# Cross attention on one core: batch 0's keys by block products, the setup in a written order, and two reads moved

## The chip, the cores and the metric

The kernel runs on one core of a Trainium2 chip. The metric is the time of one execution on the device in microseconds (us); three runs of the kernel before took 945.8, 946.26 and 946.75 us, so the median is 946.26 us. An engine of the core executes its own list of instructions in order; the engines meet only at semaphores. TensorE (PE, with its weight loads PEld) multiplies, VectorE (DVE), ScalarE (ACT) and GpSimd (POOL) work on elements, SyncE (SP) issues most of the transfers.

## The reference

For each of 16 batches, with `x` of 100 rows by 640, `enc` of 718 rows by 384 and `ca` of 4 rows by 384:

```python
query = x @ Wq;  keyt = enc @ Wk;  valt = enc @ Wv          # 8 heads of 80
hs = mha(query, keyt, valt)                                # softmax over 718 keys
ca_q1 = einsum('btc,th->bch', ca, Wq_ca)[:, indices]
ca_hs1 = mha(ca_q1, x, x)                                  # keys and values are x
ca_hs2 = mha(ca_hs1 @ Wq, ca @ Wk_ca, ca @ Wv_ca)          # 4 keys
out = (hs + ca_hs2) @ Wout + b_out + x
```

All is fp32.

## The kernel before, in words

The program is unrolled over the 16 batches. The keys of a batch are kept transposed in `kT` (5 chunks of 128 rows, three thirds of 240 columns), its values in `vs` (six blocks of 120 keys, two halves of four heads each).

Two ways of multiplying a batch's `enc` with a weight exist. The plain way takes all the partial products: `chunk_keys` makes one chunk of keys from 3 thirds by 3 parts of `enc`, nine products of 240 columns (L558), and `first_values` makes one block of values, half by half (L375). The other way, `Keys` and `Values`, multiplies the 3 by 3 parts of `enc` with 3 by 2 parts of the weight by 15 block products instead of 18 (`V_PLAN`, `K_PLAN`). It needs sums of parts: `enc_sums` makes 13 sums per batch on GpSimd (L500), `weight_sums` makes 12 sums per weight (L521). `Blocks.go(n)` issues the next n products (L434 for values, L465 for keys); after each product the bank's running sum is copied to its place by ScalarE (L407) or added there by VectorE (L405), and only then may the next product go into that bank. The fifth chunk of the keys is always made the plain way (`last_keys`).

**The setup** (L266 to L1104) is ordered by the tile scheduler, except for transfers marked `in_order`. SyncE loads `enc` of batch 0 (thirds 1 and 2), `cat`, `Wk_ca`, `Wq` transposed (L295), third 0 of `enc`, `x` transposed, `cas`, `Wk` transposed in nine transfers (`load_packed`, L302), `Wq` (L308) and `Wv_ca` (L309); ScalarE's queue loads `Wv` (L282). TensorE makes four blocks of batch 0's values (L375), the small keys `k2` (L1005) and from them `m` (L1028), the first `y_ps` (L739), the transposes of `Wk` (L1051), batch 0's keys the plain way (`first_keys`, L558), `va` (L1083) and the first queries (L534). Banks of PSUM come from three pools of two: `psumk`, `psum1`, and pairs of banks; `psum` alternates between the first two. VectorE masks `k2` (L1017), copies `m` out (L1036), sorts `Wq` into place (L1062, L1069) and makes the weight sums (seven and five of Wk, seven of Wv). GpSimd builds masks and expands `m` (L711, `keys`), then forms the first products of the second attention (L774, L781).

**The loop** (L1116) runs in an order written out by hand (`manual_schedule`, L1115). Batch b makes scores in three tiles `st[0]` to `st[2]` of two key blocks each (L613; copies L630 and L624), a running maximum (L1150), then subtracts (L1138) and exponentiates (L1146) each tile. Between them TensorE makes the products of values b and keys b+1. In batch 0 two blocks of values are still made the plain way, and GpSimd makes the last five sums of Wv (L1205). Then `a_ps` (L1301) multiplies the exponentials with the values: two groups of four heads, head by head, each over all six key blocks, in two column parts. The result is divided by the row sums. In batch 1 the second attention's part is added to batch 0's result by one VectorE instruction (L1166), which stands between the scores' maxima; then `last.transpose()` (L1210, L916) turns that sum for the last projection.

Of the kernel before, what the change touches and what calls it, by code (L numbers as in the profile page):

```python
# [132 lines left out]
def kernel(  # L133
# [62 lines left out]

    def hsT_tile(name):
        return main.tile([P, HC, P], F32, tag="hsT", name=name, bufs=2)
# [81 lines left out]
    for g in range(2):  # L280
# [6 lines left out]
    load_first(0, CC, 2, slice(0, KT))  # L287
    tokens = vb_tile("tokens")
# [3 lines left out]
    in_order(nc.sync.dma_start(out=wkca_sb, in_=wkca.rearrange("(c p) n -> p c n", p=P)))  # L292
    wqt_sb = wout_sb
    wkt_sb = kT.rearrange("p c u k -> p c (u k)")
    in_order(nc.sync.dma_start(out=wqt_sb, in_=wqt.rearrange("(c p) r -> p c r", p=P)))  # L295
    load_first(0, CC, 0, slice(0, KT))
# [4 lines left out]
    load_packed(  # L301
        lambda **ends: in_order(nc.sync.dma_start(**ends)), wkt_sb[:, :, :CAD], wkt  # L302
    )
# [45 lines left out]
    m_sb = [t[:, : B * HT] for t in (hs_tile("m_0"), xn_tile("m_1"), xn_tile("m_2"))]  # L349
# [60 lines left out]
    class Values(Blocks):  # L410
# [17 lines left out]
        def product(self, at, f, first, last):  # L428
# [4 lines left out]
            for j in range(2):  # L433
# [3 lines left out]
                    wv_sb[:, W_AT[f]],  # L437
# [43 lines left out]
    def enc_sums(enc):  # L481
# [3 lines left out]
        for out, left, right, op in (  # L485
            (at(11), raw(3, 2), raw(3, 3), ALU.add),
# [5 lines left out]
            (at(7), raw(2, 3), raw(3, 1), ALU.add),  # L492
# [9 lines left out]
    def weight_sums(engine, w, late):  # L502

        at = lambda f: w[:, W_AT[f]]
        raw = lambda c, g: w[:, 2 * (c - 1) + g - 1]
        for out, left, right in (
            (at(5), raw(2, 2), raw(1, 2)),
            (at(14), raw(2, 1), raw(2, 2)),
            (at(7), raw(3, 2), at(5)),
            (at(3), raw(1, 1), at(7)),  # L510
            (at(13), raw(3, 1), at(7)),
        ) if late else (
            (at(0), raw(1, 2), raw(1, 1)),
            (at(1), raw(2, 1), raw(3, 1)),
            (at(2), raw(1, 1), raw(2, 2)),
            (at(6), raw(2, 1), raw(1, 1)),
            (at(10), raw(3, 1), raw(2, 2)),
            (at(11), raw(2, 2), raw(3, 2)),
            (at(12), raw(3, 2), raw(3, 1)),
        ):  # L520
            engine.tensor_tensor(out, left, right, ALU.subtract)  # L521
# [8 lines left out]
    def queries(p, xT, tiles, n):  # L530
        qp, qz = tiles
        q_ps = psum(f"q_ps_{p}_{n}")
# [42 lines left out]

    def first_keys(enc):
        for n in range(HC - 1):
            banks = [psum(f"kT_ps_0_{n}_{k}") for k in range(2)]
            weights = [wk_sb[:, 2 * c + n % 2, n // 2] for c in range(CC)]
            chunk_keys(n, banks, weights, enc)  # L580
        last_keys(0, enc)
# [136 lines left out]
    class Second:  # L718
# [135 lines left out]
        def values2(self, behind=None):  # L854

            b, p2, vb = self.b, self.p2, self.vb
            self.hs2 = main.tile([S, H], F32, tag="hs2", name=f"hs2_{b}")
# [24 lines left out]
    class Last:  # L882
# [26 lines left out]
        def transpose(self, chunks=[(0, HC)]):  # L909
            b, hs = self.b, self.hs  # L910
            if not self.t_ps:
                self.t_ps = psumk(f"hst_ps_{b}")
# [83 lines left out]

    for i in (1, 4, 2, 5):
        first_values(i, enc, (act, dve))
# [14 lines left out]
    for n, heads in enumerate(HEADS):  # L1013
# [10 lines left out]
        )  # L1024
    for c in range(HC):
# [10 lines left out]
        copied = nc.vector.tensor_copy(  # L1036
# [6 lines left out]
    summed = second.products()  # L1043
# [3 lines left out]

    for c in range(HC):
        w_ps = psum(f"w_ps_{c}")
        for cc in range(CC):  # L1050
            nc.tensor.transpose(  # L1051
                w_ps[:, cc * P : (cc + 1) * P], wkt_sb[:, c, cc * P : (cc + 1) * P], ident
            )
        act(
            wk_sb[:, c % 2 : 6 : 2, c // 2] if c < HC - 1 else wk4,
            w_ps[:, : CC * P].rearrange("p (a n) -> p a n", a=CC),
        )

    with tc.issue_after(summed.ins):
        for c in range(HC):  # L1060
            for u in range(2):
# [317 lines left out]
```

## Time and profile before

| what | us |
|---|---|
| median of three runs | 946.26 (945.8 to 946.75) |
| the profiled execution | 945.6 |
| its span, first to last instruction | 943.9 |
| PE busy in it | 935.4 |
| granted TensorE clock | 0.999 |
| DVE, POOL, ACT busy | 680.7, 626.0, 361.8 |
| start of the first scores (L613) | 60.24 |

The profile is of one execution. Its span leaves out 1.7 us that the device time includes. Times of places are in us from the span's start. A product in fp32 stands in the trace as two matmul records, so "x4" in a row of products is two products. Durations of matmuls overlap in the records; how long one takes in a chain is read from starts, or from the chain of work that ended last, where each piece has its own share of time.

### The profile page before, as it was taken

To read this page: it belongs to the slowest core of one execution; us is meant where nothing else is said; L and a number is where in the kernel's file an instruction comes from. 1 tells how busy PE (TensorE), PEld (TensorE's weight loads), DVE (VectorE), ACT (ScalarE), POOL (GpSimd) and SP (SyncE) were. 2 spreads that over 40 slices of the span, in tenths; PEclk is the share of its full clock that TensorE was granted. 3 is DMA by queue.
4 is the path that set the end of the run, shared out by engine and by line. 5 is a ranking of instruction groups with operands and counts; after the bars stand their busy time and mean duration, and the time that the engine had idled before them with its cause. 6 is when DMAs were issued, how large, how long until landed. Compare 5 with 4: busy or idle time off the path is not lost.

```text
span 943.9 us, 25613 instructions
## 1 busy us (share of the span) xinstructions
PE 935.4 (99%) x11215; PEld 796.8 (84%) x11215; DVE 680.7 (72%) x1083; ACT 361.8 (38%) x598; POOL 626.0 (66%) x570
## 2 busy tenths in 40 slices
PE   9999999999999999999999999999999999999998
PEld 6997879788797888978789887987989888897866
DVE  1869794877929778595965959579693886949683
ACT  1234433524324244433424434244431534334241
POOL 4649978776737766595872948657694576848523
PEclk9999999999999999999999999999999999999999
DMA  8822014040320404004050030403113030210200
GB/s 269 268 95 87 3 48 135 1 130 3 88 65 1 116 2 118 23 2 130 1 151 3 28 91 1 138 2 94 38 38 115 1 111 8 57 55 1 94 8 29
DMA packets 45367, 62.48 MB, mean 66 GB/s; under 512 B 13448, under 2 KB 37320, under 8 KB 43656
## 3 DMA queue, kind: packets, MB, share of 16 engines
q1 hardware_dynamic: 41720, 42.97, 15.3%
q0 software_dynamic: 2512, 16.72, 6.0%
q8 instruction: 88, 1.44, 0.7%
q10 hardware_dynamic: 1024, 1.15, 0.4%
q14 instruction: 23, 0.19, 0.1%
HBM read 55.26 MB, written 5.57 MB: 64 GB/s over the span
## 4 chain that ended last, share of the span: by engine, by line
PE 95%; DVE 3%; ACT 1%; DMA 0%; issue 0%; POOL 0%; ACTq 0%; DVEq 0%
PE s_ps L613 12%; PE a_ps L1301 12%; PE v_psA L434 10%; PE v_psB L434 9%; PE kT_ps L558 7%; PE k_psA L465 7%; PE q_ps L534 7%; PE o_ps L944 7%; PE k_psB L465 6%; PE v_psC L434 3%; PE k_psC L465 2%; PE v_psD L434 2%; PE v_psE L434 2%; PE y_ps L739 2%; PE v_ps L375 1%; PE k_psE L465 1%
## 5 line engine op out<-in xcount | busy, mean ns | idle before, releaser
L774 POOL TENSOR_TENSOR e<-ca,g 100x800 f32<-100x800 f32 x64 | 99.5, 1565 | 132.4 <-DVE most L1150 128.7
L863 POOL TENSOR_TENSOR hs<-vb,p 100x640 f32<-100x640 f32 x64 | 105.0, 1650 | 40.1 <-DVE p L849 32.0
L870 POOL TENSOR_TENSOR hs<-hs,hs 100x640 f32<-100x640 f32 x48 | 115.1, 2398 | 3.8
L1301 PEld LDWEIGHTS a_ps<-vs,st 120*64 120x64 f32 (+3 forms) x3072 | 109.0, 125 | 6.9 <-issue 5.5
L1301 PE MATMUL a_ps<-vs,st 120*64 120x81 f32 (+3 forms) x3072 | 112.1, 234 | 1.0 <-ACT st L1146 1.0
L434 PE MATMUL v_psA<-wv_sb,enc 128*120 128x320 f32 x360 | 112.0, 434 | 0.0
L1138 DVE TENSOR_TENSOR st<-st,over 120x1600 f32<-120x1600 f32 x48 | 108.2, 2255 | 0.0
L500 POOL TENSOR_TENSOR enc<-enc 128x240 f32<-128x240 f32 x135 | 99.2, 749 | 7.1
L630 ACT COPY st<-s_ps 120x800 f32<-120x800 f32 x64 | 49.7, 829 | 135.9 <-PE s_ps L613 135.9
L613 PE MATMUL s_ps<-qp,kT 32*120 32x100 f32 x3072 | 97.4, 263 | 0.0
L613 PEld LDWEIGHTS s_ps<-qp,kT 32*120 32x120 f32 x3072 | 94.7, 179 | 1.6 <-issue 0.2
L781 POOL TENSOR_TENSOR e<-e,e 100x800 f32<-100x800 f32 x48 | 92.3, 1923 | 3.8
L434 PE MATMUL v_psB<-wv_sb,enc 128*120 128x320 f32 x300 | 93.1, 433 | 0.0
L465 PE MATMUL k_psA<-enc,wk_sb 128*128 128x240 f32 x360 | 87.6, 366 | 0.0
L1312 DVE RECIPROCAL rs<-a_ps 100x4 f32<-100x4 f32 x32 | 5.8, 182 | 112.9 <-PE a_ps L1301 112.9
L434 PEld LDWEIGHTS v_psA<-wv_sb,enc 128*120 128x120 f32 x360 | 64.5, 183 | 23.0 <-issue 0.5
L1150 DVE TENSOR_TENSOR most<-most,st 120x800 f32<-120x800 f32 x64 | 65.7, 1027 | 23.6 <-ACT st L624 22.5
L1146 ACT ACTIVATE st<-st 120x1600 f32<-120x1600 f32 x48 | 73.8, 1539 | 23.2 <-DVE st L1138 23.2
L465 PEld LDWEIGHTS k_psA<-enc,wk_sb 128*128 128x128 f32 x360 | 68.3, 190 | 16.7
L500 POOL TENSOR_TENSOR enc<-enc,rest 128x240 f32<-128x240 f32 x45 | 33.9, 752 | 68.3 <-DMA rest<-in_enct 36.0
L434 PEld LDWEIGHTS v_psB<-wv_sb,enc 128*120 128x120 f32 x300 | 54.8, 183 | 22.1 <-DVE vs L405 0.4
L465 PE MATMUL k_psB<-enc,wk_sb 128*128 128x240 f32 x300 | 73.1, 366 | 0.0
(137 smaller groups left out, 1765.7 us busy)
## 6 DMA issues: line engine op xcount, KB each, us to landing
vb<-va_d POOLq DMA_DIRECT2D x16, 1000.0 KB, 7.3
enc<-in_enct SPq DMA_DIRECT2D x30, 240.0 KB, 3.8
enc<-in_enct SPq DMA_DIRECT2D x15, 360.0 KB, 3.5
xT<-in_xt SPq DMA_DIRECT2D x8, 500.0 KB, 4.6
rest<-in_enct SPq DMA_DIRECT2D x31, 120.0 KB, 6.1
xn<-in_x SPq DMA_DIRECT2D x11, 320.0 KB, 5.3
out<-xn SPq DMA_DIRECT2D x11, 320.0 KB, 3.1
ca<-in_cas SPq DMA_DIRECT2D x16, 156.2 KB
```

Source lines behind the costliest of these rows:

```text
L434: nc.tensor.matmul(at[0][j][:KN, : H // 2], a_form(self.enc, f)[:, j * KN : (j + 1) * KN], wv_sb[:, W_AT[f]], start=first, stop=last, skip ...
L465: nc.tensor.matmul(at[:, i * KT : (i + 1) * KT], wk_sb[:, W_AT[f], i], a_form(self.enc, f), start=(first and i == 0), stop=last, skip_grou ...
L500: nc.gpsimd.tensor_tensor(out, left, right, op)
L534: nc.tensor.matmul(q_ps[:, : 2 * S].rearrange("p (j s) -> p j s", j=2), wq_sb[:, c, n * P : (n + 1) * P], xT[:, :, c, :], start=(c == 0), ...
L613: nc.tensor.matmul(s_ps[r][:n, 256 * a + lo : 256 * a + hi], kT[rows, c, u, j * KN : (j + 1) * KN], rhs, start=(a == 0 and c == 0), stop=( ...
L774: first = nc.gpsimd.tensor_tensor(to, self.ca[:, t, :].unsqueeze(1).to_broadcast([S, NH, S]), g[:, :, t].unsqueeze(2).to_broadcast([S, NH, ...
L781: nc.gpsimd.tensor_tensor(e, e, to, ALU.add)
L863: first = nc.gpsimd.tensor_tensor(to, vb[:S, t, :].rearrange("p (h d) -> p h d", h=NH), p2[:, :, t].unsqueeze(2).to_broadcast([S, NH, D]), ...
L870: nc.gpsimd.tensor_tensor(sums, sums, to, ALU.add)
L1138: return nc.vector.tensor_tensor(st[i], st[i], top.over[:KN].unsqueeze(1).to_broadcast([KN, 2, ROWS]), ALU.subtract,)
L1146: nc.scalar.activation(st[i], st[i], AF.Exp, scale=SCALE)
L1301: nc.tensor.matmul(a_v[lo:hi, h % 4], st[i // 2][: KEYS[i], i % 2, h * S + lo : h * S + hi], block(i, h // 4)[: KEYS[i], h % 4], start=(i ...
```

## The change

- `Wq` transposed is loaded by ScalarE's queue, issued after the fourth copy of values; SyncE loads third 0 of `enc` before `cat`, and `Wk` transposed ahead of `x` transposed, `cas` and `Wq`.
- The hand-written order begins before the first values. All their copies are ScalarE's.
- `enc_sums` for batch 0 stands in the setup, and `f=7` is made first. All 12 sums of Wv are made by VectorE in the setup; three of them (5, 14, 7) go to spare room (`wv_there`, in `bias` and a tile of `xn`), and ScalarE copies them into `wv_sb` late in batch 1, after which the bias is loaded. GpSimd's five sums in batch 0 are gone.
- The transposes of `Wk` come before `m`, ScalarE copies `m` out, all sums of Wk follow on VectorE at once, then the sorting of `Wq`.
- Batch 0's keys are made by 15 block products, `k0.go(3)`, then `y_ps`, then `go(4)`, `va`, and two after each of the first four query chunks; `last_keys` stands before the last query chunk. `va` and the queries take pairs of banks.
- In the first group of `a_ps` the order is by tiles of scores: all four heads over `st[0]`, then `st[1]`, then `st[2]`.
- In batch 1 the addition of `hs2` stands after `y_ps` of the next batch, and the transposes after three value and three key products, in a bank of `psum1`.

```diff
     load_first(0, CC, 2, slice(0, KT))
+    load_first(0, CC, 0, slice(0, KT))
...
+    load_packed(
+        lambda **ends: in_order(nc.sync.dma_start(**ends)), wkt_sb[:, :, :CAD], wkt
+    )
     wqt_sb = wout_sb
-    in_order(nc.sync.dma_start(out=wqt_sb, in_=wqt.rearrange("(c p) r -> p c r", p=P)))
-    load_first(0, CC, 0, slice(0, KT))
...
-    load_packed(
-        lambda **ends: in_order(nc.sync.dma_start(**ends)), wkt_sb[:, :, :CAD], wkt
-    )
...
+    room_v = xn_tile("wv_there")
+    wv_there = {5: bias[:, : H // 2], 14: bias[:, H // 2 :], 7: room_v[:, : H // 2]}
...
-    q_ps = psum(f"q_ps_{p}_{n}")
+    q_ps = get(f"q_ps_{p}_{n}")
...
+    ctx.enter_context(tc.manual_schedule(engines=engines))
     for i in (1, 4, 2, 5):
-        first_values(i, enc, (act, dve))
+        first_values(i, enc, (act, act))
+        if i == 4:
+            nc.scalar.dma_start(out=wqt_sb, in_=wqt.rearrange("(c p) r -> p c r", p=P))
+    enc_sums(enc)
+    weight_sums(nc.vector, wv_sb, there=wv_there)
...
+    for c in range(HC):
+        w_ps = psum(f"w_ps_{c}")
...
+    weight_sums(nc.vector, wk_sb)
...
-        copied = nc.vector.tensor_copy(
+        nc.scalar.copy(
             m_sb[c].rearrange("p (b h t) -> p h b t", h=NH, t=T),
...
+    k0 = Keys(0, enc)
+    k0.go(3)
+    second.products()
     second.copy()
     second.scores1()
     keys(load_m(1))
...
-    first_keys(enc)
-    weight_sums(nc.vector, wk_sb, True)
+    k0.go(4)
...
-    va_ps = psum("va_ps")
+    va_ps = bank("va_ps")
...
     for n in range(HC):
-        queries(0, xT, tiles, n)
-    nc.gpsimd.dma_start(out=bias, in_=bout[0].partition_broadcast(P))
+        queries(0, xT, tiles, n, bank)
+        k0.go(2)
+        if n == HC - 2:
+            last_keys(0, enc)
...
-        if b == 1:
-            nc.vector.tensor_tensor(last.hs[:S], last.hs[:S], last.hs2, ALU.add)
         st.append(scores(b, 2, tiles))
 
         now.softmax2()
         if b + 1 < B:
             second.products()
             second.copy()
+        if b == 1:
+            nc.vector.tensor_tensor(last.hs[:S], last.hs[:S], last.hs2, ALU.add)
...
-            weight_sums(nc.gpsimd, wv_sb, True)
...
-            last.transpose()
+            if b > 1:
+                last.transpose()
...
+            if b == 1:
+                last.transpose(get=psum1)
...
+            if b == 1:
+                for f in list(wv_there):
+                    nc.scalar.copy(wv_sb[:, W_AT[f]], wv_there.pop(f))
             second.load()
+            if b == 1:
+                nc.gpsimd.dma_start(out=bias, in_=bout[0].partition_broadcast(P))
...
-            for h in range(4 * g, 4 * g + 4):
...
+            order = [(h, i) for h in range(4 * g, 4 * g + 4) for i in range(len(KC))]
+            if g == 0:
+                order.sort(key=lambda at: at[1] // 2)
+            for h, i in order:
```

## The prediction

> **What bounds the kernel now.** I read the page first: busy time of each engine, then the granted clock by slice.
>
> ```profile
> PE 935.4 (99%) x11215; PEld 796.8 (84%) x11215; DVE 680.7 (72%) x1083; ACT 361.8 (38%) x598; POOL 626.0 (66%) x570
> ...
> PEclk9999999999999999999999999999999999999999
> ```
>
> TensorE is busy for 935.4 of 943.9 us at full clock. So only two things can save time: fewer products, or less of the 8.5 us in which PE is idle or winding up. Next I read what PE waited for over the whole span:
>
> ```profile
> PE hst_ps L916 <- DVE hs L1166: 1.3, 1, 1.3
> PE idle_ps L994 <- DVE idle L991: 1.1, 1, 1.1
> PE a_ps L1301 <- ACT st L1146: 1.0, 1, 1.0
> PE m_ps L1028 <- DVE wq L1017: 0.5, 1, 0.5
> PE y_ps L739 <- POOL m L711: 0.4, 1, 0.4
> PE k_psC L465 <- DVE kT L405: 0.3, 1, 0.3
> ```
>
> All of these lie in the first 112 us; batches 2 to 15 have no wait of PE to win. Apart from the start (1.1) they add up to 3.5 us. Last, the chain of work in the setup:
>
> ```profile
> 21.27 6.91 PE m_ps L1028 x50
> ...
> 31.66 18.23 PE kT_ps L558 x90
> 49.89 1.76 PE va_ps L1083 x12
> 51.65 8.66 PE q_ps L534 x50
> ```
>
> From 30 us to the first scores (60.24) PE runs without a gap, so what is taken from PE there is won, as long as nothing it needs is late.
>
> **Fewer products.** `first_keys` makes 4 chunks of 9 products and the fifth chunk 9 more: 45 products, 90 records, 18.23 us, so 0.405 us each. The 36 become 15 plan steps of 2 products, 30. A block product has the same 240 columns and the same price: a row of two, k_psA x4, takes 0.81 in the chain of batch 1. Six products fewer: **-2.43 us**. This is certain if the waits do not grow.
>
> **Waits removed.**
> - `m` waits 0.47 for the masks of `k2`, `y_ps` 0.40 for GpSimd. Now the transposes of Wk (15 records, some 2.05 us by their starts) stand between `k2` and `m`, and the masks need 1.2; between `m` and `y_ps` stand three plan steps (2.43), and the last expansion of `m` needs ScalarE's copy (0.69 on VectorE before) and 0.3 on GpSimd. **-0.87**.
> - `a_ps`: before, PE ran 16 records on `st[0]` and `st[1]` and stood 1.02 for `st[2]`. With all four heads over two tiles first, 64 records at 36.4 ns (6.41 us for 176) lie ahead of `st[2]`: from 92.51 to 94.84, and that tile was ready at 94.27. **-1.02**, with 0.5 of cover. The pairs of column parts alternate as before, so I put the new order itself at nothing; it touches 16 groups of 3.5 us, and one per cent either way would be 0.56.
> - `hst_ps`: the transposes now follow 5.7 us of products, and the addition (1.31) ends well within that. But PE then is 1.3 us nearer to VectorE's additions: that of v_psA ended at 120.56 and its next product began at 121.86, so the cover becomes about nil. I keep **-1.1** of 1.31; 0.5 at worst.
> - The wait of k_psC (0.34) stays: the order there is the same.
>
> **Waits added.** Three, all in the setup.
>
> (1) *The last transfer of Wk transposed.* In the built program each transfer waits for the one eight places before it on the shared semaphores; the ninth of Wk (the fifth chunk) waits for Wq transposed. Behind it on SP stand `x` transposed, `cas`, `Wq`, `Wv_ca`; on PE the fifth transpose, then `m` and all that follows. ScalarE issues Wq transposed after its fourth copy (12.48 + 0.42): about 12.9, instead of 8.45. Now the rates:
>
> ```profile
> 10.00:15.00 5.00, 5.00 (x21) 3.36 (x20) 0.49 (x1) 0.85 (x2) 2.24 (x6) 1.00 0.99 377
> ...
> 20.00:24.00 4.00, 3.53 (x48) 3.39 (x45) 1.91 (x6) 0.00 (x0) 0.29 (x1) 1.00 0.94 204
> 24.00:28.00 4.00, 4.00 (x32) 4.00 (x32) 2.07 (x3) 0.00 (x0) 0.98 (x3) 1.00 0.39 103
> ```
>
> The last column is GB/s. Ahead of Wk transposed are `enc` 1.11, Wv 0.98, `cat` 0.10 and Wk_ca 0.98 MB, 3.17 in all; 1.91 had moved by 10 us (191 GB/s), the rest at 377 ends at 13.4. Then come Wk transposed (0.98) and Wq transposed (1.64) together. Here a rule speaks against the change: the Trainium skill, "DMA: Bandwidth & Descriptors", "Issuing engines are not separate DMA queues", says that transfers started on different queues run on the same 16 engines and interleave, so a second queue saves only issue time. So ScalarE's queue brings nothing by itself, and Wq transposed slows Wk. By the rule the sum of bytes counts: 2.62 MB at 377 is 7.0 us, ending at 20.4. By the row in which Wk's packets ran (204, transfers into 32 partitions) it is 12.8 us, ending at 26.2. I take the first: in that row SP stood still, 5.2 us for Wq transposed and 2.3 for `x`, so few transfers were in flight, while now seven are issued ahead. The ninth is then issued at 20.4 and lands 2.6 to 3.2 us later (what the 60 KB loads took): 23.0 to 23.6. PE, done with `k2` at 20.85, has done four transposes by 22.5. Wait 0.5 to 1.1: **+0.8**. By the row it would be 6.6.
>
> (2) *VectorE's additions to kT.* These stand behind the sums of Wk and the sorting of Wq. Sums: 12 by 0.345 from about 23.2, to 27.4; `k0` begins at 30.9 and is covered. Sorting: it took 13.2 us (30.36 to 43.58), because GpSimd's long products ran alongside:
>
> ```profile
> 35.69 0.21 DVE L1069 COPY wq_sb<-wq 128x128 f32<-128x128 f32 x1
> 35.83 1.82 DVE L1062 COPY wq_sb<-wq 128x256 f32<-128x256 f32 x2
> 37.57 1.90 DVE L1069 COPY wq_sb<-wq 128x128 f32<-128x128 f32 x1
> ```
>
> The same copy takes 0.21 or 1.90: a blocked one waits for one whole GpSimd instruction (1.6 to 1.9). Now those products come after `g`, which VectorE makes after the sorting; only the expansions of `m` (0.3 each) run beside it. So 3.3 us alone, 5 with them, to about 32.4, if Wq has landed: 1.64 MB and 0.68 for `x` and `cas` behind 20.8, at 377, is 29. `y_ps` ends at 34.6, so 2 us of cover. What remains is that A's third product waits for VectorE's addition of its second: **+0.2** (0 to 0.8).
>
> (3) *The pair for the first scores.* Queries now take pairs of banks. The built program shows the second pair of the scores waiting for ScalarE's two masked copies of the last query chunk. They took 0.74 after that chunk's end (60.34 to 61.08); before, scores began at once, since queries lay in other banks. PE can do four records, so **+0.75** (0.3 to 1.2).
>
> What is put at nothing: VectorE's 12 sums of Wv (0.40 each, 8 to 13 us; masks needed at 20.85; doubled, still in time); GpSimd's 13 sums of batch 0 (0.75 each, 11.9 to 21.7; first needed at 30.9; at twice the price the last ends near 31, and the expansions are the next late thing); four more copies and `m` on ScalarE, which was 13% busy or less there; its three copies in batch 1, ahead of `st[2]`, behind which 8.5 us of queries stand on PE; the bias load after them on GpSimd, needed in batch 2. The sums of Wv gone from GpSimd (7.34 us in batch 0) were on no path of PE: nothing.
>
> **The sum**: -2.43 - 0.87 - 1.02 - 1.1 + 0.8 + 0.2 + 0.75 = -3.67. The first scores begin about 1.3 us earlier in effect; the rest comes in batches 0 and 1. The profiled execution would take 945.6 - 3.67 = 941.9 (its span 940.2); it lay 0.66 below the median, so the median becomes 942.6. With all favourable ends the gain is 2.43 + 0.87 + 1.02 + 1.31 + 0.33 - 0.3 = 5.7, 940.6.
>
> **Rivals.**
> - *A: the setup gives it back.* If the two transposed weights end at 23 instead of 20.4, wait (1) is about 3.3: 942.6 + 2.5 = 945.1. For it: the window at 204. Against: the window at 377.
> - *B: VectorE late.* Additions to kT now end near 53, then the first softmax's 8.3 us beside GpSimd's sums of batch 1, so VectorE is free near 62, and it is needed for the maxima at 63.6; before, it idled 5.6 us there. If it is 1.5 us late, exponentials are late, `a_ps` loses its 1.0 again and batch 1 0.8: 944.4.
> - *C: slower.* Wq transposed lands at 26.2 or later, by the row. Then the ninth transfer lands at 29.1 and PE stands 6.6: -3.67 + 5.8 = +2.1, 948.4. It decides from a landing of Wq transposed at about 26. A pause that long may cost more: the skill's "TensorE: Matmul & The Clock Gate", "HAM oscillation — how this bites in real kernels", tells of a lower clock after idle gaps of over some 3.4 us; the longest gap here is 1.3 at a clock of 0.999, so no row shows it.
>
> **Chances.** Forecast 0.62, A 0.15, B 0.12, C 0.11. I call a change of over 0.2% (1.9 us) told apart from none, about what a measurement of this kernel can do: below 944.4 faster, above 948.2 slower. Faster: 0.60 of the forecast, 0.05 of A, half of B: 0.71. Slower: most of C, 0.09. The rest, 0.20, is within. The range 940.8 to 946.0 holds the forecast's bounds, A and B.
>
> **What would show it.** 30 products at L470 and none of the plain chunks but the fifth before the first scores; no wait of `hst_ps` on L1174 nor of `a_ps` on the exponentials; a wait of w_ps on the load of Wk near 22.5, of under 1.1; a wait of s_ps on ScalarE of some 0.75; first scores near 59. Wrong would make it: a wait of w_ps over 3 us, rows of `wq_sb` copies of 1.6 us or more, `a_ps` longer than 36.4 ns a record in its first groups, or a wait of PE in the later batches.

## The result and the profile after

The changed kernel takes 953.09 us (median of four runs, 950.3 to 954.28); the kernel before, 946.09 beside it. The ratio is 1.0071 with an interval of 1.0059 to 1.0083, so it is 5.6 to 7.9 us slower. The profiled execution took 953.05 us, with a span of 951.3 (before 943.9). The page of the changed kernel, engines and clock:

```profile
PE 937.2 (99%) x11203; PEld 798.1 (84%) x11203; DVE 672.5 (71%) x1088; ACT 367.7 (39%) x608; POOL 624.5 (66%) x578
...
PEclk9799999999999999999999999999999999999999
```

There are 12 records fewer on PE, as six products fewer must give, and yet PE is busy 1.8 us longer. The clock row says why: its second slice, about 24 to 48 us, has a 7. PE did less work, but some of it at a lower clock. The waits of PE in the changed kernel:

```profile
PE w_ps L1040 <- DMA kT<-in_wkt: 6.8, 3, 3.3
...
PE k_psE L470 <- DVE vs L410: 0.9, 1, 0.9
PE s_ps L612 <- ACT qz L552: 0.5, 1, 0.5
...
PE k_psA L470 <- DVE kT L410: 0.2, 1, 0.2
```

The waits of `hst_ps`, `a_ps`, `m_ps` and `y_ps` are gone, as intended. In their place PE stands 6.8 us for Wk transposed, in three pieces: 3.27 us before the transposes that start at 23.73, 0.50 before those at 25.73, and 3.05 before the fifth chunk's at 30.30. What the loads waited for is in SyncE's own queue, for the first 45 us:

```profile
SPq L299 <- DMA wout_sb<-in_wqt: 8.1, 1, 8.1
...
SPq L299 <- DMA tokens<-in_wkca: 3.6, 1, 3.6
```

L299 is the loading of Wk transposed. Its seventh transfer stood 3.6 us for the landing of `Wk_ca` (16.76), so that the seventh and eighth were issued at 16.78 and 17.54, and its ninth stood 8.1 us for that of Wq transposed. The chain of work that ended last shows the second of these from end to end (start, duration, what):

```profile
12.14 13.78 DMA wout_sb<-in_wqt
...
25.94 4.31 DMA kT<-in_wkt
...
30.30 0.90 PE w_ps L1040 x3
31.20 9.12 PE m_ps L1051 x50
```

Wq transposed was under way for 13.78 us; of its 640 packets only 14 began in the last two of them. Only then was the ninth transfer issued, of 192 KB; it took 4.31 more, and `m` could begin at 31.20 instead of 21.27. The 50 records of `m` then took 9.12 us, where they took 6.91 before. The windows of the same kernel (last three columns: granted clock, share of DMA, GB/s):

```profile
10.00:15.00 5.00, 5.00 (x20) 3.40 (x19) 3.13 (x7) 1.28 (x3) 4.88 (x13) 1.00 1.00 274
15.00:18.00 3.00, 3.00 (x13) 2.05 (x12) 0.00 (x0) 0.85 (x2) 2.84 (x5) 1.00 1.07 181
18.00:20.00 2.00, 2.00 (x54) 1.55 (x54) 0.00 (x0) 0.43 (x1) 1.84 (x4) 1.00 1.05 288
20.00:24.00 4.00, 0.73 (x18) 0.62 (x15) 1.22 (x5) 0.00 (x0) 3.15 (x5) 0.83 0.87 275
24.00:28.00 4.00, 2.75 (x12) 1.98 (x10) 0.20 (x1) 1.92 (x4) 0.00 (x0) 0.50 0.11 17
...
32.00:36.00 4.00, 4.00 (x17) 4.00 (x17) 1.52 (x7) 0.59 (x1) 0.41 (x1) 0.50 1.01 386
36.00:40.00 4.00, 4.00 (x31) 4.00 (x31) 2.04 (x9) 1.76 (x3) 1.03 (x3) 0.97 1.02 397
```

The DMA engines are fully busy from 10 to 20 us and yet move only 181 to 288 GB/s; from 24 to 28 us, with the end of Wq transposed and the start of the ninth transfer, next to nothing moves. The clock falls while PE stands: by the trace's list of clocks it is one half from 22.62 to 36.27 us. From 32 to 36 us PE makes 17 records, where the next four microseconds hold 31.

**Where the time went.** The first scores start at 67.73 instead of 60.24, 7.5 us later. Of that: waits for Wk +6.8; `m`, mostly at half clock, +2.2 (9.12 - 6.91); the transposes without their waits 3.9 us instead of 1.7, +2.3; the wait of `m` -0.5; from the end of `m` to the end of `y_ps` 0.96 us instead of 1.82, -0.9; the keys' pieces of the chain 16.1 us instead of 18.23, -2.1; the small keys start 0.3 earlier. These sum to +7.5. Then batch 0 is 0.8 us shorter (39.60 instead of 40.40), batch 1 as long as before (58.74 and 58.62), and batches 2 to 15 are 0.6 longer, for a cause that stays open.

That batch 1 is no shorter, though `hst_ps` waits no more, is told by the chain through it:

```profile
117.36 1.15 DVE hs L1174
118.51 0.91 DVE most L1152
119.42 0.02 issue
119.44 1.38 DVE most L1152
...
128.94 0.66 DVE kT L410
...
130.95 1.08 PE k_psE L470 x4
```

The addition that was moved (`hs`, 1.15 us) still stands on VectorE ahead of two maxima. From there the chain of what ended last stays with VectorE for over ten microseconds, to its additions to `kT` at 128.94 and to `vs` at 130.52; PE's product of k_psE, which stood 0.92 us for the latter, begins at 130.95. The wait of 1.30 us was not removed; as 0.25 and 0.92 it moved from the transposes to the additions.

### The profile page after: what moved, and what is told of

It reads as the page before. It is cut to its first block, busy times and chain, and to the rows that moved or that the text cites. A ratio compares the mean times of both kernels' runs of the same rounds, so it can differ in the third digit from the quotient of the medians.

```text
span 951.3 us, 25636 instructions
## 1 busy us (share of the span) xinstructions
PE 937.2 (99%) x11203; PEld 798.1 (84%) x11203; DVE 672.5 (71%) x1088; ACT 367.7 (39%) x608; POOL 624.5 (66%) x578
## 4 chain that ended last, share of the span: by engine, by line
PE 93%; DVE 3%; DMA 2%; issue 0%; ACT 0%; ACTq 0%; DVEq 0%
PE s_ps L612 12%; PE a_ps L1313 12%; PE v_psA L439 10%; PE v_psB L439 8%; PE k_psA L470 8%; PE q_ps L540 7%; PE o_ps L943 7%; PE k_psB L470 6%; PE kT_ps L564 6%; PE v_psC L439 3%; PE k_psC L470 3%; PE y_ps L738 2%; PE v_psD L439 2%; PE v_psE L439 2%; DMA wout_sb<-in_wqt 1%; PE k_psE L470 1%
## 5 line engine op out<-in xcount | busy, mean ns | idle before, releaser
L1313 PEld LDWEIGHTS a_ps<-vs,st 120*36 120x36 f32 (+3 forms) x3072 | 109.2, 125 | 5.6 <-issue 5.5
L1313 PE MATMUL a_ps<-vs,st 120*36 120x81 f32 (+3 forms) x3072 | 111.9, 233 | 0.0
L505 POOL TENSOR_TENSOR enc<-enc 128x240 f32<-128x240 f32 x144 | 104.9, 738 | 7.5
L439 PE MATMUL v_psA<-wv_sb,enc 128*120 128x320 f32 x352 | 109.6, 434 | 0.0
L470 PE MATMUL k_psA<-enc,wk_sb 128*128 128x240 f32 x384 | 93.7, 367 | 0.3 <-DVE kT L410 0.2
L470 PEld LDWEIGHTS k_psA<-enc,wk_sb 128*128 128x128 f32 x384 | 72.5, 190 | 17.8 <-POOL e L780 0.7
L470 PE MATMUL k_psB<-enc,wk_sb 128*128 128x240 f32 x320 | 77.9, 366 | 0.0
L540 PE MATMUL q_ps<-xT,wq_sb 128*128 128x200 f32 x400 | 69.7, 333 | 0.0
```

The costliest lines, as they stand in the source:

```text
L439: nc.tensor.matmul(at[0][j][:KN, : H // 2], a_form(self.enc, f)[:, j * KN : (j + 1) * KN], wv_there.get(f, wv_sb[:, W_AT[f]]), start=first ...
L470: nc.tensor.matmul(at[:, i * KT : (i + 1) * KT], wk_sb[:, W_AT[f], i], a_form(self.enc, f), start=(first and i == 0), stop=last, skip_grou ...
L505: nc.gpsimd.tensor_tensor(out, left, right, op)
L540: nc.tensor.matmul(q_ps[:, : 2 * S].rearrange("p (j s) -> p j s", j=2), wq_sb[:, c, n * P : (n + 1) * P], xT[:, :, c, :], start=(c == 0), ...
L1313: nc.tensor.matmul(a_v[lo:hi, h % 4], st[i // 2][: KEYS[i], i % 2, h * S + lo : h * S + hi], block(i, h // 4)[: KEYS[i], h % 4], start=(i ...
```

## The experiments

The theory was: the loss is one of order. Two weights share the DMA engines, the order in which they land is not the order in which PE needs them, and the wait that follows lowers the clock as well; the block products and the loop's new order are innocent. The rivals were that the narrow transfers of Wk are too slow whatever the order, that the clock costs nothing of its own, and that the loop part is worth nothing.

**1. Wq transposed behind Wk transposed**, on SyncE:

```diff
+    in_order(nc.sync.dma_start(out=wqt_sb, in_=wqt.rearrange("(c p) r -> p c r", p=P)))
...
-        if i == 4:
-            nc.scalar.dma_start(out=wqt_sb, in_=wqt.rearrange("(c p) r -> p c r", p=P))
```

> The changed kernel, but Wq transposed is issued by SyncE behind the nine transfers of Wk transposed, so the two don't run at once and no transfer of Wk waits for it. Theory (the two streams slowed each other on the same engines, and the ninth transfer was held by Wq transposed): the wait of the first transposes falls from 3.3 us to under 1, that of the fifth from 3.0 to under 0.5, and a wait of m for Wq transposed of 2 to 3 us appears at some 25 us; the clock stays at 1.00 or nearly; time 945 to 947. Rival (the nine transfers into 32 partitions are slow by themselves): the transposes still wait 3 us and more, Wq transposed lands later than 26, time 952 or more.

It took 948.9 us (948.63 to 949.12, six runs), ratio to before 1.0029 [1.0017, 1.0040]. The waits of its PE, and its windows:

```profile
PE m_ps L1050 <- DMA wout_sb<-in_wqt: 3.5, 1, 3.5
...
PE w_ps L1039 <- DMA kT<-in_wkt: 0.3, 1, 0.3
```

```profile
24.00:28.00 4.00, 0.89 (x4) 0.92 (x5) 3.72 (x11) 0.16 (x1) 0.00 (x0) 0.68 1.04 379
28.00:32.00 4.00, 4.00 (x17) 4.00 (x17) 0.63 (x3) 0.59 (x1) 0.29 (x1) 0.50 1.02 341
```

And the chain of work that ended last:

```profile
9.54 9.08 DMA tokens<-in_wkca
...
19.81 7.16 DMA wout_sb<-in_wqt
...
27.11 9.33 PE m_ps L1050 x50
```

4.2 us of the 7 are won back by this one line, less than the theory asked (945 to 947). Wk is there just in time; now `m` waits 3.5 us for Wq transposed, and the half clock follows that wait as well. The chain shows why Wq transposed is late: SyncE could issue the eighth transfer of Wk only when `Wk_ca` had landed (18.62), then the ninth, and Wq transposed behind it. From 16 to 20 us the DMA engines had a share of 0.31 and moved 72 GB/s; Wq transposed alone then went at 379. So what one weight gains in order, the other loses. The rival is not excluded: with no Wq transposed beside them, Wk's packets took 107 ns on average from 14 to 18 us, where 65 is the least. Nor does the run, which changes the queue and the order of Wq transposed together, tell these two apart.

**2. Wk transposed in five transfers into 128 partitions** (instead of nine into 32 or fewer):

```diff
-    for r, u in [(r, u) for r in range(RG) for u in range(2)]:
-        load(
-            out=to[32 * r : 32 * r + 32, 2 * u : 2 * u + 2],
-            in_=rows[r, u, :64].rearrange("(j p) n -> p j n", j=2),
-        )
+    for u, j in [(u, j) for u in range(2) for j in range(2)]:
+        load(out=to[:, 2 * u + j], in_=rows[:, u, 32 * j : 32 * j + 32])
```

> The changed kernel, but Wk transposed comes in five transfers into all 128 partitions instead of eight into 32 and one into 128, the same bytes. Theory with narrow transfers as the ones that load few engines and drag Wq transposed along: all of Wk lands by about 20, Wq transposed by about 21, waits of the transposes under 1 us in all, clock 1.00, time 944 to 946. Rival (two queues at once are slow whatever their shape): waits of 4 us and more stay, time 950 or more. Here the fifth transfer also doesn't stand behind Wq transposed on a semaphore, so the first wait (3.3) tells the shape, the last one (3.0) may go for either reason.

It took 953.79 us, ratio 1.0083 [1.0069, 1.0097]: nothing won, and `w_ps` waits 8.6 us. By the time that is the rival. But in these transfers the outermost dimension of the source is 4, and from 16 to 30 us mostly 19 to 45 of their packets began in a microsecond, 65 to 126 ns each, as if few engines took part. The Trainium skill, "DMA: Bandwidth & Descriptors", "Rules for kernel authors", says that an outermost dimension of fewer than 16 keeps a transfer to at most that many engines; the run agrees. So this did not test what it was meant to test, the width of the destination, and leaves theory and rival where they were.

**3. PE kept at work**: zero products ahead of the first and the fifth transpose (their results are unused).

```diff
+    warm_ps = bank("warm_ps")
+    warm(14)
     for c in range(HC):
+        if c == HC - 1:
+            warm(14)
```

> The changed kernel with 14 products of zeros (about 3.0 us) ahead of the first and 14 ahead of the fifth transpose of Wk, so TensorE isn't idle while it waits for the load. Theory (the idle time lowered the clock to half from 24 to 36 us): the clock stays at 1.00, m takes 6.9 us again instead of 9.1, time 949.5 to 951, 2 to 3.5 us less than the changed kernel. Rival (m was slow because of what it reads or of the transfers beside it): m stays at 9.1, time within 0.5 of the changed kernel or more.

The median is 951.42 us, but the four runs lie between 948.86 and 954.58, ratio 1.0067 [1.0050, 1.0084]: by the times not told apart from the changed kernel. The zero products kept the clock up in only two of the four: these were granted 1.000 on average and took 948.86 and 950.76, the other two 0.998 and took 952.08 and 954.58 (the changed kernel's four: 0.993 to 0.996). The profiled execution was the shortest of them (span 946.5). Its clock is 1.00 in every window from 20 to 40 us, `m` began at 29.37, and the first scores started at 63.38, 4.35 us earlier. It shows that the clock follows PE's idling, not the size of the gain.

**4. The loop part alone**: the setup of before, with the new order of `a_ps`, and the addition and transposes of batch 1 moved as in the change.

```diff
+            order = [(h, i) for h in range(4 * g, 4 * g + 4) for i in range(len(KC))]
+            if g == 0:
+                order.sort(key=lambda at: at[1] // 2)
...
+            if b > 1:
+                last.transpose()
...
+            if b == 1:
+                last.transpose(get=psum1)
```

> The kernel before with only the two changes in the loop: the first group of the product with V by tiles of scores, and in batch 1 the later sum with the transposes after three products of each. As predicted: the waits of a_ps (1.0) and hst_ps (1.3) go, 944.0 to 944.6 (0.1 to 0.5 us returned by VectorE's additions in batch 1). Rival (what the changed kernel's trace suggests: batch 1 gives it back in two new waits of 0.25 and 0.9): 945.0 to 945.4.

946.36 us (21 runs), ratio 1.0004 [0.9997, 1.0010]: neither the theory's number nor the rival's. The waits of `a_ps` and `hst_ps` are gone, and a new one stands first among the causes in its profile:

```profile
PE k_psA L465 <- POOL enc L500: 2.2, 1, 2.2
```

Batch 2's keys wait for GpSimd's sums of `enc`: with the transposes out of the way, PE comes to them sooner than their pair, the seventh in GpSimd's list, is made. The profiled execution (948.86) is one of the slowest of the 21: right after this wait its clock was one half for 3.41 us, and its first values were slow, so that the first scores started at 61.67.

**5. The loop part, with that pair first in the list:**

```diff
+            (at(7), raw(2, 3), raw(3, 1), ALU.add),
...
-            (at(7), raw(2, 3), raw(3, 1), ALU.add),
```

> The changed kernel's loop part alone, as before (a_ps by tiles, the first sum and its transposes later, setup as it was), now with its order of GpSimd's sums as well: the pair of batch 2's first key chunk is added first. Theory (the 2.2 us that the earlier loop-only run lost at batch 2's keys came from that pair being added seventh, and the later sum wins little because batch 1 waits for VectorE's additions instead): the wait of k_psA on GpSimd falls under 0.5 us, a_ps's 1.0 us is won, of the 1.1 us of hst_ps at most 0.5; 944.6 to 945.4. Rival (the loop part is worth nothing, whatever the order of the sums): 945.8 to 946.4, with another wait of 1 us or more in batches 1 or 2.

943.69 us (11 runs), ratio 0.9977 [0.9968, 0.9985]. One line in the order of 13 sums decides whether the loop part is worth 2.2 us, by the ratio, or nothing. It is worth slightly more than I expected. Its profiled execution was one of its longer ones (945.89), and shows waits of 0.92 and 0.75 us on VectorE's additions in batch 1; run 12 returns to them.

**6. Run 1 with PE kept at work** by zero products ahead of `m`:

```diff
+    warm_ps = bank("warm_ps")
+    for _ in range(16):
+        nc.tensor.matmul(warm_ps[:, :P], idle, idle, start=True, stop=True)
```

> The kernel of the run with Wq transposed issued behind Wk transposed, plus 16 products of zeros ahead of m (extra work, its result unused) that fill the time in which TensorE waits for Wq transposed. Theory (the clock: a wait of 3.5 us makes m and what follows run at a clock of one half for several us): the clock stays at 0.95 or above in every stretch from 20 to 40 us, m takes 6.9 us instead of about 9, the first scores come about 2.2 us earlier than in that run (61.6 instead of 63.85), and the time is 946.2 to 947.0. Rival (the lower clock costs nothing that the later stages would not give back): 948.4 to 949.2, as without the zeros.

947.81 us, ratio 1.0013 [1.0005, 1.0021], with runs from 945.34 to 950.23; the interval overlaps that of run 1. All 20 executions were granted 0.999 or 1.000, where run 1's had 0.996 to 0.998. In the profile the clock is 1.00 in every window from 20 to 40 us, and `m` takes 6.84 us instead of 9.33 with no other change in what it computes. About half of the expected gain shows in the median. The profiled execution, at 949.59 one of the slow ones, tells where a gain can go: the loads ended later (the small keys waited 1.2 us for `Wk_ca`, Wk transposed another 1.3), so `m` began 2.0 us later than in run 1. The half clock has a price of its own, 2.5 us for `m`; that the loads' scatter explains the other executions is not shown, since each run has one trace.

**7. The whole change with loads and setup in the order of before**: SyncE loads Wq transposed ahead of Wk, and `m` precedes the transposes.

```diff
-        if i == 4:
-            nc.scalar.dma_start(out=wqt_sb, in_=wqt.rearrange("(c p) r -> p c r", p=P))
+    in_order(nc.sync.dma_start(out=wqt_sb, in_=wqt.rearrange("(c p) r -> p c r", p=P)))
...
+    for c in range(HC):
+        w_ps = psum(f"w_ps_{c}")
...
+    weight_sums(nc.vector, wk_sb)
+    last_keys(0, enc)
```

> The whole change, but with the order of the loads and of TensorE's setup as before: Wq transposed by SP ahead of Wk transposed, m first, then Wk's transposes, their sums, the last key chunk, then y and the queries. The keys by block products, the sums of Wv in setup and the loop's new order stay. Theory (the loss is the order in which the two weights are needed against the order in which they land, with the clock behind it, and not the block products): no wait of w_ps or m_ps above 1 us, clock 0.95 or above from 20 to 40 us, first scores at 59.5 to 60.2, 944.0 to 945.3. Rival (the block products' setup itself has no cover, since Wk's transposes now stand ahead of the last keys): TensorE waits 2 us or more for Wk transposed or its copies whatever the order, 947 or above.

944.32 us (22 runs), ratio 0.9983 [0.9974, 0.9991]: 8.8 us less than the changed kernel. No wait on Wk or Wq transposed is left, the clock is 1.00 throughout, and the first scores start at 57.92, 2.3 us before those of the kernel before. So the loss lay in the order, that of the loads with their queue and that of PE's setup, which this run turns back together, and not in the block products. These waits are left in its profile where gain was expected:

```profile
PE z_ps L801 <- issue: 1.2, 2, 1.0
...
PE kT_ps L565 <- ACT wk L1060: 1.0, 1, 1.0
PE k_psE L471 <- DVE vs L411: 0.9, 1, 0.9
PE m_ps L1039 <- issue: 0.5, 1, 0.5
PE s_ps L613 <- ACT qz L553: 0.5, 1, 0.5
```

Those of `kT_ps`, for ScalarE's copy of the last transposed chunk of Wk, and of `m` come with the old order of the setup; no run takes them away.

**8. Two of these waits attacked**: the last query chunk in the other pool of PSUM, and batch 1's addition on GpSimd.

```diff
-        queries(0, xT, tiles, n, bank)
+        queries(0, xT, tiles, n, bank if n < HC - 1 else psum1)
...
-            nc.vector.tensor_tensor(last.hs[:S], last.hs[:S], last.hs2, ALU.add)
+            nc.gpsimd.tensor_tensor(last.hs[:S], last.hs[:S], last.hs2, ALU.add)
```

> As the run with the order of before, and two edits more: the last chunk of batch 0's queries in a bank of the other pool of PSUM, and batch 1's second addition to its first sum on GpSimd instead of VectorE. Theory (the 0.45 us ahead of the first scores is a wait for the eviction of the query chunk whose bank they take, and the 0.25 and 0.92 us of batch 1's keys are waits for VectorE, which stands in that addition): the three waits fall under 0.2 us each, and the time is 1.0 to 1.6 us below that run, 943.0 to 944.3. Rival (the waits move to the next instruction on the same engine): within 0.4 us of that run.

947.07 us, ratio 1.0008 [0.9999, 1.0016]: 2.75 above run 7 and worse than the rival's number. In the profile both waits went, and `hst_ps` now stands 2.44 us for GpSimd's addition, while 0.85 us of an unexplained stop appear in the scores. GpSimd was no free place. That profile is of one of the two fastest of 14 executions (945.0, clock 1.000). The other twelve were granted 0.997 or 0.998 and took 946.05 to 949.1; one stretch at half clock like that of run 4, 3.41 us, would make 0.998. So the new stop seems to cost most executions the clock as well, which no trace shows.

**9. The stop without a releaser.** In the profiles of runs 6, 7 and 8 PE stops for 0.85 to 1.02 us with the releaser "issue" (nothing that the profile shows), at recorded instruction 961 or 1218 of its stream. I lengthened its program at the start by 84 instructions:

```diff
-    for _ in range(5):
+    for _ in range(2):
         nc.tensor.matmul(idle_ps[:, :P], idle, idle, start=True, stop=True)
+    for _ in range(24):
+        nc.tensor.matmul(
+            idle_ps[:32, :32], idle[:32, :32], idle[:32, :32], start=True, stop=True
+        )
```

> The kernel of the run with the order of before, with TensorE's program 84 instructions longer at its very start (two of the five zero products that open it stay, 24 small zero products are added in the time in which it waits for its first weights; their results are unused). In three profiles TensorE stands 0.85 to 1.02 us in the middle of the small products of batch 0's first scores and first softmax with no releaser, at recorded instruction 961 or 1218 of its stream, 257 apart, and each packet of the instruction queue has 16,384 bytes. Theory (it stands there for the next block of its own instructions, whose fetch is late beside the loads): the blocks now end 84 instructions earlier in the work, the wait of z_ps at 67.5 us goes or falls under 0.3 us, and the time is 0.7 to 1.1 us below that run: 943.2 to 943.7. Rival (the wait belongs to those products themselves): it stays at the same product, 944.0 or above.

944.69 us, ratio 0.9981 [0.9973, 0.9989]: no gain in time, against the theory's number and within the rival's. The profile splits it. The stop of `z_ps` is gone, and batch 0 takes 39.98 us instead of 40.86; but the first values began 1.3 us late behind my zero products and ran slowly, so that the small keys start at 20.44 instead of 18.31. What I won in one place I had paid in another.

**10. The shift and the other pool for the last query chunk** together:

```diff
-        queries(0, xT, tiles, n, bank)
+        queries(0, xT, tiles, n, bank if n < HC - 1 else psum1)
```

> As the shifted kernel, with the last chunk of batch 0's queries in a bank of the other pool of PSUM. Theory: the 0.45 us of s_ps ahead of the first scores goes, since those scores no longer take the bank of a chunk that has still to be evicted: first scores without a wait above 0.1 us, 942.7 to 943.3. Rival (the wait moves to the next scores or to an instruction block): within 0.2 us of the shifted kernel.

944.64 us, ratio 0.9983 [0.9977, 0.9990], the same as run 9: the rival again. The 0.45 us of the first scores is gone, and 0.26 and 0.34 us appear behind it, on ScalarE's copies of scores and on VectorE.

**11. The addition and transposes later still**, in addition to run 10:

```diff
-        if b == 1:
-            nc.vector.tensor_tensor(last.hs[:S], last.hs[:S], last.hs2, ALU.add)
...
-            if b == 1:
-                last.transpose(get=psum1)
...
             exponential(1)
             vv.go(1)
             kk.go(2)
+            if b == 1:
+                nc.vector.tensor_tensor(last.hs[:S], last.hs[:S], last.hs2, ALU.add)
             both(1)
             both(1)
+            if b == 1:
+                last.transpose(get=psum1)
```

> As the run before it, with batch 1's second addition to its first sum moved on VectorE from ahead of its maximum to behind its second exponential (where VectorE stands idle for 0.2 to 0.5 us at a time in the profile, at 133 to 136 us), and the first sum's transposes to behind the next keys. Theory (batch 1's 0.25 and 0.92 us are waits for VectorE's additions to keys and values, which stand behind that 1.23 us addition): both waits fall under 0.2 us, 941.6 to 942.4. Rival (the transposes and the projection then end the batch late): 942.8 or above, with a new wait of hst_ps or o_ps.

943.35 us (five runs), ratio 0.9963 [0.9951, 0.9976]. That is above what I expected and within the rival's number, though without the rival's new wait: batch 1 takes 57.21 us instead of the 58.74 of run 7, with no wait of PE above 0.1 us. The theory of VectorE's queue holds: the addition had to leave the stretch in which VectorE is never idle, not the place of one product.

**12. The same for the loop part alone** (run 5 with the diff of run 11).

> The changed kernel's loop part alone (the setup of before, with its keys), with the pair of batch 2's first key chunk added first by GpSimd, and with batch 1's addition and transposes of the first sum moved later still, as in the run before this. Theory (waits for VectorE of 0.92 and 0.75 us in batch 1 were what was left of the loop part): 942.5 to 943.3, under the 943.7 of the loop part with the pair alone. Rival (that profile was one of its slower executions, and its usual one has no such waits): 943.4 to 944.0.

943.93 us, ratio 0.9971 [0.9959, 0.9984], the same as run 5: the rival. Its batch 1 takes 57.60 us and has one wait of 0.21 us. So run 5's usual execution, which is as fast, can hardly have had the waits of its profiled one.

**13. Run 7 with the addition and transposes later** (the diff of run 11), without shift or pool.

> The whole change with the loads and TensorE's setup in the order of before, and batch 1's addition and transposes of the first sum moved behind its second exponential; nothing else. Theory: the 0.25 and 0.92 us of batch 1 go and more with them (57.2 us for batch 1 instead of 58.7, as in the shifted run), the 0.98 us of z_ps in batch 0 stays: 1.2 to 1.5 us below the 944.3 of the order alone, 942.6 to 943.2. Rival (batch 1's gain belongs to the shift and is given back): 943.8 to 944.6.

943.15 us (nine runs), ratio 0.9970 [0.9960, 0.9979]. As expected, 1.2 us under run 7 (the intervals just overlap), with batch 1 at 57.81 us; the stop was longer in its profiled execution. Its stretch of small products:

```profile
66.38 0.39 PE L801 MATMUL z_ps<-y,e 100*32 100x33 f32 x22
68.54 0.56 PE L801 MATMUL z_ps<-y,e 100*4 100x33 f32 x42 [1.77 <-issue]
```

PE stops for 1.77 us inside one group of 64 small products that otherwise takes 0.75 us.

**14. Run 13, with the shift made out of the opening zero products**:

```diff
-    for _ in range(5):
-        nc.tensor.matmul(idle_ps[:, :P], idle, idle, start=True, stop=True)
+    for _ in range(24):
+        nc.tensor.matmul(
+            idle_ps[:32, :32], idle[:32, :32], idle[:32, :32], start=True, stop=True
+        )
```

> As the run beside it, with the opening five zero products (2.5 us) replaced by 24 small ones (2.77 us in the shifted profile), which makes TensorE's program 76 instructions longer and its start about 0.3 us later. Theory (the 0.98 us is a wait for a block of instructions and goes when the block ends elsewhere): z_ps without a wait above 0.3 us, 0.4 to 0.8 us below the run beside it, 941.8 to 942.7. Rival (the first values are late again, as in the shifted run, which lost 2.1 us there): 943.2 or above.

943.27 us (eight runs), ratio 0.9970 [0.9959, 0.9980]: no gain over run 13. The stop is gone once more and batch 0 takes 40.00 us instead of 41.68, and once more the setup is 2.0 us late. This time the first values began only 0.1 us later than in run 7; they ran at half speed for longer. First run 14, then run 7, in the same window of PE:

```profile
3.82 1.42 PE L381 MATMUL v_ps<-wv_sb,rest 128*120 128x320 f32 x2
...
7.89 1.27 PE L381 MATMUL v_ps<-wv_sb,rest 128*120 128x320 f32 x2
```

```profile
3.69 1.42 PE L381 MATMUL v_ps<-wv_sb,rest 128*120 128x320 f32 x2
...
6.91 0.70 PE L381 MATMUL v_ps<-wv_sb,rest 128*120 128x320 f32 x2
```

Two products take 1.27 to 1.42 us until about 9 us in the one, and 0.70 from 6.9 us on in the other. The five large zero products look like more than filler; how far the traces bear that out is said below, under the slow start.

Runs 5, 11, 12, 13 and 14 beat the kernel before by 2.2 to 3.5 us by their ratios, runs 7, 9 and 10 by 1.6 to 1.8; the intervals of the five overlap, so none is shown to be the best.

## Why the prediction was wrong

It said 942.6; the time is 953.09, above the range and on the other side. Its rival C had the mechanism, with a chance of 0.11.

- **The step that failed: "(1) The last transfer of Wk transposed", +0.8.** The dependence was read rightly: the ninth transfer was issued in the moment in which Wq transposed landed. Its size was wrong: 6.8 us, and with it came the prediction's own sign, a wait of `w_ps` over 3 us. What failed is the rate of 377 GB/s. The loads ahead, put to end at 13.4, ended with `Wk_ca` at 16.76, and held the seventh transfer of Wk; so the transposes, four of which should have been done by 22.5, began only at 23.73. While both weights were in flight the engines were full or nearly so (shares of 0.87 to 1.07) at 181 to 288 GB/s. So 377, the rate of one stretch with other transfers, was not the rate of these. The row of 204 GB/s had given a wait of 6.6 and a landing of 26.2, and it was 25.93. I had both ends, and put the row aside because "few transfers were in flight, while now seven are issued ahead". Six of Wk had been issued by 13.1 us, with Wq transposed beside them, and the rate stayed low. That the row came so near is in part luck, for its 13.4 was wrong as well. The skill's rule that queues share the engines was right, but I used it to add bytes at a rate that the two weights never reached together. Also the ninth transfer took 4.3 us, not 2.6 to 3.2: it carries 192 KB, and those figures were of loads of 60.
- **The clock, not priced at all.** I named the rule and left it out of the sum of C, as no row showed it. It cost `m` 2.2 us and lies in the 2.3 of the transposes: most of the way from C's 948.4 to 953.09. Run 6 against run 1 gives 2.5 us of `m` for it.
- **"-1.1" for `hst_ps`** was mis-sized within the full change: batch 1 went from 58.62 to 58.74. The prediction's own remark that the cover would become about nil was the whole story, and it took 0.5 as the worst. Run 11 shows the gain to be there once the addition leaves VectorE's busy stretch.
- **Keys, -2.43: right in kind, and partly spent later.** The chain shows 2.1 of it, and with the old order the first scores come 2.3 us earlier (run 7; the small keys began 0.5 earlier there, and the wait of `kT_ps` took 0.95). In the time it doesn't show in full: run 13 lies 0.8 us under run 12, which keeps the old keys, and that is not told apart. In run 13's profile PE's stop takes 1.8 us and `s_ps` 0.45.
- **`a_ps`, -1.02: right.** The wait is gone, and batch 0 is 1.1 us shorter in run 5; the new order itself costs nothing (111.9 us busy in all). **`m` and `y_ps`, -0.87: right** by the waits. **`s_ps`, +0.75**: 0.45, within its bounds. **Rival B and the sorting of `Wq`**: no copy to `wq_sb` took longer than 0.44 us, and `a_ps` did not lose its gain again. (The loads behind the ninth transfer, 2.32 MB at 377 after 20.8, would end at 27; the prediction has 29.)
- The chances rested on one choice between two rates that lay 5.8 us apart. Both ends belonged in the range, which ended at 946.0; without a term for the clock it would still have ended below 953.09.

## What to carry to other kernels

When two loads are to run together, take the rate from the row in which transfers of their own shape ran, and ask of every transfer which earlier landing it waits for; then load in the order in which PE needs the data. A wait of PE of 2 to 3.5 us can cost more than itself, when what follows runs at half clock; the mean granted clock of every execution tells whether the profiled one is typical. Before a step is moved on an engine that is never idle, find the stretch in which it is, for a move inside the busy stretch only moves the wait.

## What the runs showed of the hardware

- **The clock.** It changes in steps: the four stretches at half clock amid the traces last 3.41 us (run 4), 6.83 (run 1), 10.24 (run 2) and 13.65 (the changed kernel), all multiples of 3.41. The fall does not wait for a gap of that length. It came 2.2 us after PE's last record in the changed kernel, 1.8 in run 1, and in run 4 just behind a stop of 2.20. In the step of 3.41 us before each of the four falls PE was busy for 0.5 to 1.25 us; the least busy step that left the clock at 1.00 has 1.74 (run 2), and in run 8, with a stop of 2.44, it is 1.94. So where a stop lies in the steps seems to decide; that may be why nine of run 4's 21 executions were granted 0.997 or 0.998 (946.26 to 949.23 us) and twelve 0.999 or more (945.08 to 946.74). Full clock came back only behind a step in which PE was busy throughout: at 36.27 in the changed kernel, 5 us after `m` began. The Trainium skill, "TensorE: Matmul & The Clock Gate", "HAM oscillation — how this bites in real kernels", puts the limit at idle gaps of some 3.4 us; here 2.2 was enough.
- **A slow start that the clock row doesn't show.** The trace's list of clocks begins where full clock sets in, at 6.73 us in run 7 and 10.24 in run 14; the row gives 1.00 for what stands before, though products took twice their time there. With the five large zero products it began at 4.95 to 7.43 in eleven profiles and at 10.24 in the twelfth, run 4; with the small ones at 7.81 to 10.95 in four. In runs 9 and 10 PE was busy throughout the step before, in part with small products, and no full clock followed. So products of 32x32 seem to count for less than those of 128x128; no run isolates it.
- **Packets of two loads.** In the changed kernel a packet of Wk transposed (1,536 bytes) took 65 ns on average in the microsecond from 13 us, then 98, 124, 154 and 177 up to 18, with packets of Wq transposed (2,560 bytes) beside it from 15 on; those took 126 to 268 up to 21, where packets of that size took 108 from 10 to 14 in the kernel before. Two weights slow each other. But Wk's narrow transfers do so among themselves too: 107 ns in run 1 from 14 to 18, with only the last packets of `Wk_ca` beside them, and 117 from 22 to 24 us in the kernel before.
- **PE stops at its own instructions.** The page of the changed kernel lists PE's instruction queue among the DMA queues (packets, MB, share):

```profile
q8 instruction: 88, 1.44, 0.6%
```

That is 16 KB a packet. The stops lay 257 recorded instructions apart, at the same two numbers in four profiles, and went when the stream before them was made 84 or 76 longer. The Trainium skill, "Runtime: NRT & Kernel Launch", "Instruction fetch mechanics", says that instructions come in blocks of 256, the next fetched while one runs, and that this is mostly hidden. Here it wasn't: small products use up a block in under 4 us. In the profiles with a stop PE went on 1.25 to 1.57 us after the end of an instruction packet; in the others it came to record 1218 from 1.45 to 2.40 us after one, without a stop. The packet ahead of the stop at 1218 had begun 2.4 to 3.1 us after PE passed record 961; in the kernel before, with next to no loads, it was 0.3. So the wait for a block rests on these times and on the shift. That loads delay the block is not shown: they ran beside all four (171 to 238 GB/s), but in the changed kernel the packet came after 0.2 us beside 259 GB/s. Shorter stops without a releaser, of 0.2 to 0.4 us, lie at 1218 in run 2 and, in the changed kernel and runs 4, 5, 7, 12 and 13, a multiple of 256 records behind 1218, to within one.
